# GpSimd takes over a quantiser's rounding, and two pieces of work are asked for earlier

## The chip, the cores and the metric

The kernel runs on one core of a Trainium2 chip. The core has a matrix engine (TensorE, PE in the profile, with its weight loads as PEld), VectorE (DVE), ScalarE (ACT), GpSimd (POOL) and SyncE (SP, which here issues DMA transfers). Each engine runs its own list of instructions strictly in order, so an instruction that waits holds up everything behind it in that list. The metric is the device time of one execution in microseconds (us).

## The reference

The input is x, two sequences of 4096 tokens with 512 channels. Two layers follow each other, and each adds two branches to its input.

```python
xn = _layernorm(x, axis=-1)
x = x + _L0_attn_ref(xn, ...) + _L0_ffn_ref(xn, L0_ffn_weight, L0_ffn_bias)
xn = _layernorm(x, axis=-1)
x = x + _L1_attn_ref(xn, ...) + _L1_ffn_ref(xn, ...)
```

In layer 0 the "attention" is two projections (w1, v1), a depthwise convolution of three taps with SiLU, a state-space recurrence over the tokens, a gate and a projection w2. Its "ffn" is a product of two quantised operands: every block of 32 numbers is divided by a scale and rounded to the nearest number of a 6-bit grid.

```python
scales = jnp.maximum(jnp.max(jnp.abs(blocks), axis=-1) / FP6_E2M3_MAX, eps)
q = _nearest_on_grid(blocks / scales[..., None], _GRID)
xd = (xq * xs[..., None]).reshape(x2.shape)   # wd likewise
out = xd @ wd.T + bias
```

In layer 1 the attention is linear: q and k through ReLU, the sums of k times v and of k over all tokens, a product with q, a quotient, and a layernorm of the result plus its input. Its ffn mixes each token with the one before it, `xk = mu_k * x + (1.0 - mu_k) * x_prev` and xr likewise, and computes `sigmoid(xr W_r) * (square(relu(xk W_k)) W_v)`.

## The kernel before, in words

Tokens are cut into blocks of 512, sixteen in all and eight in each sequence; a block holds four tiles of 128 tokens. Channels come in four groups of 128. Most operands are 128 x 512 numbers in 32-bit floats. The profile's times show these stages:

- the conv stage, to about 402 us: block by block the layer norm, the two projections, the taps (L479) and the stores for the recurrence. Beside the blocks, 24 of the 64 tiles and the 4 rows of the ffn weight are quantised (`beside`, `beside_block`);
- the recurrence, to about 620 us;
- the mixed blocks of sequence 0 (about 623 to 890 us): the gate, the products with w2 and with the quantised weight, the sum into x (L799 empties a bank of accumulators into x), the turned x for layer 1, and k (L894) with its running sum over tokens on GpSimd (L853). Eight more tiles are quantised here;
- the outer sums of k and v (about 890 to 992 us), with eight tiles (`early`) beside them; GpSimd prepares operands for them at L934;
- the pairs (about 992 to 1192 us): q and then k of layer 1's ffn for two blocks at a time, with products by seven quarter products (`seven`, L1072). ScalarE's L1079 copies a finished bank away, so that TensorE can go on; L1108 and L1109 finish q, L1119 to L1121 finish k. The remaining tiles of sequence 1's first blocks are quantised here (`later`);
- layer 1 of sequence 0 (about 1192 to 1450 us), with four tiles of sequence 1 beside it (`ahead`, through `at_block`);
- the mixed blocks, outer sums, pairs and layer 1 of sequence 1.

To quantise a tile, ScalarE normalises it (L136, four instructions), VectorE takes the largest magnitude in each block of 32 (L187), makes the scales (L188) and their reciprocals (L192); GpSimd multiplies by the reciprocals (L193); VectorE adds a small constant and writes the sum as an 8-bit float, which does the rounding (L201); GpSimd multiplies by the scales (L202); VectorE transposes the tile (L458; L445 for a weight row). SyncE stores most of the tiles (L460). The work is a generator of four steps, which other stages call a step at a time. The tiles share a ring of eight buffers (`yv`) with other temporaries, and a single buffer (`t2q`) holds a transposed tile until its store has landed.

The mixing for W_k (`mixed_k`) takes one instruction on ScalarE (L1138) and one on VectorE (L1139) for each group of channels of each of two blocks, sixteen instructions in all. It is called from `halfway`, between the fourth and fifth of q's seven products. The mixing for W_r (L1148, L1149) comes after q.

A framework's scheduler puts the instructions into each engine's list in an order that follows the program's, and adds the waits; so a change in the program also moves instructions that it does not touch.

Of the kernel before, what the change touches and what calls it, by code (L numbers as in the profile page):

```python
# [17 lines left out]
P = 128  # L18
# [26 lines left out]
def block_kernel(ctx: ExitStack, tc: tile.TileContext, a: dict, out: bass.AP):  # L45
# [152 lines left out]
    def mx_rounded(y, s):  # L198

        q = small.tile([P, D], FP8, tag="mx_q", name="mx_q")  # L200
        nc.vector.tensor_scalar(q, y, -LOWER * GRID, None, ALU.add, saturate=False)  # L201
        nc.gpsimd.tensor_tensor(  # L202
            by_block(y), by_block(q), s.unsqueeze(2).to_broadcast([P, NQ, QB]), ALU.mult
        )
# [405 lines left out]
    def t8(shape=(P, CC, T)):  # L610
        return cl.tile(list(shape), F32, tag="t8", name="t8", bufs=7)
# [414 lines left out]
    def quarters(w):  # L1026
        return lambda i, j: w[:, 2 * j : 2 * j + 2, i * 2 * P : (i + 1) * 2 * P]
# [73 lines left out]
    def pairs(b, xnTs, wq, wk, made, kvx, later):  # L1101

        xks = {}

        def put_q(p, o, n, pm, addend):
            t = t2("q")
            if addend is not None:
                nc.vector.tensor_tensor(t, pm, addend, ALU.add)  # L1108
            nc.scalar.activation(  # L1109
                t, pm if addend is None else t, AF.Relu, bias=bq[:, o, :]  # L1110
            )
            nc.scalar.dma_start(out=qd[b * NB + 2 * p + n, o], in_=t)
            if p:
                stepped(later)

        def put_k(p, o, n, pm, addend):
            t = t2("k")
            if addend is not None:
                nc.vector.tensor_tensor(t, pm, addend, ALU.add)  # L1119
            nc.scalar.activation(t, pm if addend is None else t, AF.Relu)  # L1120
            nc.scalar.activation(t, t, AF.Square)  # L1121
            nc.scalar.dma_start(out=kd[b * NB + 2 * p + n, o], in_=t)
            if p:
                stepped(later)

        def of_q(p):
            return [lambda k, n=n: xnTs[2 * p + n][:, k, 1 : T + 1] for n in range(2)]

        def of_k(p):
            return [lambda k, n=n: xks[p][n][:, k, :] for n in range(2)]  # L1130

        def mixed_k(p):
            xks[p] = [t8(), t8()]
            for n in range(2):
                xnT = xnTs[2 * p + n]
                for c in range(CC):
                    dst = xks[p][n][:, c, :]
                    nc.scalar.activation(dst, xnT[:, c, 0:T], AF.Copy, scale=om_k[:, c, :])  # L1138
                    nc.vector.scalar_tensor_tensor(  # L1139
                        dst, xnT[:, c, 1 : T + 1], mu_k[:, c, :], dst, ALU.mult, ALU.add  # L1140
                    )

        def mixed_r(p):
            for n in range(2):
                xnT = xnTs[2 * p + n]
                for c in range(CC):
                    t = yv.tile([P, T], F32, tag="yv", name="t")
                    nc.scalar.activation(t, xnT[:, c, 0:T], AF.Copy, scale=om_r[:, c, :])  # L1148
                    nc.vector.scalar_tensor_tensor(  # L1149
                        xnT[:, c, 1 : T + 1], xnT[:, c, 1 : T + 1], mu_r[:, c, :], t,  # L1150
                        ALU.mult, ALU.add,
                    )

        NP = NB // 2
        ts = token_sums(*of_q(0))
        sq = weight_sums(quarters(wq))
        sk = None
        for p in range(NP):

            def halfway():  # L1160
                nonlocal ts_k
                if p == 0:
                    keys_values(*made, kvx)
                mixed_k(p)
                ts_k = token_sums(*of_k(p))

            ts_k = None
            seven(quarters(wq), sq, *of_q(p), ts, ("mm", "tr", "acc"), partial(put_q, p), halfway)
            if p == 0:
                sk = weight_sums(quarters(wk))  # L1170
            mixed_r(p)

            def halfway():
                nonlocal ts
                if p + 1 < NP:
                    ts = token_sums(*of_q(p + 1))

            seven(quarters(wk), sk, *of_k(p), ts_k, ("acc", "tr", "mm"), partial(put_k, p), halfway)
            del xks[p]
        while later:  # L1180
            stepped(later)

    def layer1(b, xrs, mvs, kvx, wts, at_block):
        wr, wv = wts
        for i in range(NB):
            n = b * NB + i
            at_block(i)
            qT = t8()
            nc.sync.dma_start(out=qT, in_=qd[n].rearrange("c p t -> p c t"))
            xt8 = x8()  # L1190
            xt = [xt8[:, j, :] for j in range(TJ)]
            for j in range(TJ):
                nc.sync.dma_start(out=xt[j], in_=xd1[n, j * P : (j + 1) * P])
            ka = t8()
            nc.sync.dma_start(out=ka, in_=kd[n].rearrange("c p t -> p c t"))
            xr = xrs[i]
            y = t8((P, TJ, D))
            rs = []
            for j in range(TJ):
                tj = slice(j * P, (j + 1) * P)  # L1200
                for c2 in range(2):
                    pc = bank(("tr", "mm")[j % 2])[:, 0 : 2 * (P + HG)]
                    pc = pc.rearrange("p (c m) -> p c m", c=2)
                    for c in range(2):
                        nc.tensor.matmul(  # L1205
                            pc[:, c, :],
                            lhsT=qT[:, 2 * c2 + c, tj],
                            rhs=kvx[:, 2 * c2 + c, :],
                            start=True,
                            stop=True,  # L1210
                        )
                    den = small.tile([P, 2, HG], F32, tag="den", name="den")
                    nc.vector.tensor_scalar(den, pc[:, :, P:], EPS_DEN, None, ALU.max)
                    nc.vector.reciprocal(den, den)
                    nc.vector.tensor_tensor(
                        y[:, j, c2 * 2 * P : (c2 + 1) * 2 * P].rearrange(
                            "p (c h d) -> p c h d", c=2, d=HD
                        ),
                        pc[:, :, 0:P].rearrange("p c (h d) -> p c h d", d=HD),
                        den.unsqueeze(3).to_broadcast([P, 2, HG, HD]),  # L1220
                        ALU.mult,
                    )
                xn = t2("xn")
                rescaled(xn, xt[j], mvs[:, i, j, :])
                nc.vector.tensor_tensor(y[:, j, :], y[:, j, :], xn, ALU.add)
                nc.gpsimd.tensor_tensor(xt[j], xt[j], beta, ALU.add)  # L1226
                pr = acc()
                product(
                    pr, lambda k: xr[:, k, 1 + j * P : 1 + (j + 1) * P], lambda k: wr[:, k, :]
                )  # L1230
                r = t2("r")
                nc.scalar.activation(r, pr, AF.Sigmoid)  # L1232
                rs.append(r)
            mv = small.tile([P, TJ, 2], F32, tag="mv", name="mv")
            layernorm_stats(lambda j: y[:, j, :], mv)
            for j in range(TJ):
                tj = slice(j * P, (j + 1) * P)
                nc.vector.scalar_tensor_tensor(
                    y[:, j, :], y[:, j, :], mv[:, j, 0:1], gamma, ALU.subtract, ALU.mult
                )  # L1240
                nc.vector.scalar_tensor_tensor(
                    xt[j], y[:, j, :], mv[:, j, 1:2], xt[j], ALU.mult, ALU.add
                )
                pf = acc()
                product(pf, lambda k: ka[:, k, tj], lambda k: wv[:, k, :])
                nc.vector.tensor_tensor(rs[j], rs[j], pf, ALU.mult)  # L1246
                nc.vector.tensor_tensor(xt[j], xt[j], rs[j], ALU.add)
                nc.sync.dma_start(
                    out=out[b, i * T + j * P : i * T + (j + 1) * P, :], in_=xt[j]
                )  # L1250


    mv0 = const.tile([P, NK, TJ, 2], F32, name="mv0")
    eight = banks()

# [153 lines left out]
    for b in range(B):  # L1409
# [22 lines left out]
                quantised((b + 1) * NB, j, lambda j=j: xd0[j], t2q) for j in range(TJ)  # L1432
            ]

        def at_block(i):

            if b + 1 < B:
                for _ in range(2):
                    next(ahead[i // 2])
            if b + 1 < B and i == NB - 1:  # L1440
                next_in.append(t8())
                for cc in range(CC):
                    gated(b + 1, 0, next_in[0], cc)
# [70 lines left out]
```

## Time and profile before

| what | us |
|---|---|
| median of 3 runs | 2314.48 (2311.11 to 2317.88) |
| the profiled execution | 2317.41 |
| its span in the profile | 2315.6 |
| TensorE busy | 2261.1 (98%) |
| VectorE busy | 1587.5 (69%) |
| ScalarE busy | 1024.2 (44%) |
| GpSimd busy | 544.5 (24%) |

The mean clock that TensorE was granted is 0.992 of its full speed. A busy TensorE is given in the profile by modelled ends of its instructions. A line like `PE p_mm L781 <- DVE x L799: 15.7, 5, 4.8` says that TensorE, before an instruction of line 781 that writes p_mm, stood idle 15.7 us in five waits, the longest 4.8, and that VectorE's instruction of line 799 writing x ended them. In a timeline each line has the start, the duration, engine, line, operation, the written and the read names, their shapes, and in brackets the idle time of that engine just before and what ended it; consecutive instructions of one kind may be joined in a line (x2).

### The profile page before, as it was taken

To read this page: it belongs to the slowest core of one execution; us is meant where nothing else is said; L and a number is where in the kernel's file an instruction comes from. 1 tells how busy PE (TensorE), PEld (TensorE's weight loads), DVE (VectorE), ACT (ScalarE), POOL (GpSimd) and SP (SyncE) were. 2 spreads that over 40 slices of the span, in tenths; PEclk is the share of its full clock that TensorE was granted. 3 is DMA by queue.
4 is the path that set the end of the run, shared out by engine and by line. 5 is a ranking of instruction groups with operands and counts; after the bars stand their busy time and mean duration, and the time that the engine had idled before them with its cause. 6 is when DMAs were issued, how large, how long until landed. Compare 5 with 4: busy or idle time off the path is not lost. (4 is left out here: it accounts for less than half of the span.)

```text
span 2315.6 us, 24940 instructions
## 1 busy us (share of the span) xinstructions
PE 2261.1 (98%) x7648; PEld 1269.6 (55%) x7648; DVE 1587.5 (69%) x3115; ACT 1024.2 (44%) x2019; POOL 544.5 (24%) x548
## 2 busy tenths in 40 slices
PE   7999998999989999999999999999999999999999
PEld 3444443455467676854445555567676854445554
DVE  6788678655686764577668779677764355667777
ACT  5787775555232234357652222132132246652222
POOL 0013131011343225712012112333234600001111
PEclk9999999999999999999999999999999999999999
DMA  7854643389776557524274336457557412254431
GB/s 248 295 162 150 185 152 139 125 264 320 269 211 227 178 178 229 174 86 150 96 252 160 118 138 204 164 179 240 169 160 218 146 51 96 87 209 146 145 125 57
DMA packets 291766, 399.62 MB, mean 173 GB/s; under 512 B 59057, under 2 KB 120497, under 8 KB 290609
## 3 DMA queue, kind: packets, MB, share of 16 engines
q1 hardware_dynamic: 262544, 330.91, 43.9%
q10 hardware_dynamic: 29088, 67.12, 7.6%
q8 instruction: 61, 1.00, 0.2%
q14 instruction: 73, 0.59, 0.1%
HBM read 249.42 MB, written 148.53 MB: 172 GB/s over the span
## 5 line engine op out<-in xcount | busy, mean ns | idle before, releaser
L165 PE MATMUL p_acc<-w_W_v,t 128*128 128x512 f32 x512 | 222.3, 592 | 0.0
L1226 POOL TENSOR_TENSOR x<-x,row_beta 128x512 f32<-128x512 f32 x64 | 83.2, 1300 | 590.4 <-ACT xn L136 590.4
L165 PE MATMUL p_acc<-w_W_r,xnT 128*128 128x512 f32 x448 | 201.4, 592 | 0.0
L193 POOL TENSOR_TENSOR xq<-xq,mx_rs 128x512 f32<-128x512 f32 x64 | 69.7, 1093 | 438.9 <-DVE mx_rs L192 182.4
L165 PEld LDWEIGHTS p_acc<-w_W_v,t 128*128 128x128 f32 x512 | 97.3, 190 | 122.5 <-issue 119.8
L1232 ACT ACTIVATE r<-p_acc 128x512 f32<-128x512 f32 x64 | 38.3, 598 | 261.6 <-PE p_acc L165 248.2
L853 POOL TENSOR_TENSOR ksum<-ksum,k 128x512 f32<-128x512 f32 x62 | 83.9, 1354 | 238.6 <-ACT k L895 238.5
L136 ACT ACTIVATE xq<-xq,mvi 128x128 f32<-128x128 f32 x256 | 108.2, 483 | 69.6 <-DMA xq<-in_xi 38.2
L895 ACT ACTIVATE k<-k 128x512 f32<-128x512 f32 x64 | 40.3, 630 | 196.1 <-DVE k L894 185.3
L165 PEld LDWEIGHTS p_acc<-w_W_r,xnT 128*128 128x128 f32 x448 | 80.8, 190 | 80.4 <-issue 80.4
L118 ACT ACTIVATE rs_s<-rs_v 128x4 f32<-128x4 f32 (+1 forms) x41 | 8.4, 206 | 251.2 <-DVE rs_v L116 251.1
L479 DVE SCALAR_TENSOR_TENSOR xc<-x,col_conv_w,xc 128x512 f32<-128x512 f32 x128 | 99.4, 799 | 27.0 <-ACT xc L477 15.9
L781 PE MATMUL p_mm<-w_sums,t 128*128 128x256 f32 x416 | 100.7, 398 | 14.4 <-DVE x L799 14.4
L165 PE MATMUL p_acc<-xnT,w_w_w 128*128 128x512 f32 x224 | 102.6, 601 | 2.6 <-DVE xnT L333 1.9
L165 PE MATMUL p_acc<-xnT,w_v_w 128*128 128x512 f32 x224 | 100.8, 593 | 0.1
L165 PE MATMUL p_acc<-w_Wk,xnT 128*128 128x512 f32 x224 | 100.7, 592 | 0.0
L165 PE MATMUL p_tr<-w_Wk,xnT 128*128 128x512 f32 x224 | 100.7, 592 | 0.0
L131 DVE BATCH_NORM_STATS2 st<-x 128x6 f32<-128x512 f32 x128 | 84.1, 678 | 22.9 <-DMA x<-in_x 21.9
L781 PEld LDWEIGHTS p_mm<-w_sums,t 128*128 128x128 f32 x416 | 83.1, 201 | 28.4 <-DVE x L799 16.0
L1246 DVE TENSOR_TENSOR r<-r,p_acc 128x512 f32<-128x512 f32 x64 | 43.8, 685 | 75.7 <-PE p_acc L165 75.7
L781 PE MATMUL p_acc<-w_sums,t 128*128 128x256 f32 x416 | 94.0, 379 | 0.0
L136 ACT ACTIVATE xi<-xi,mvi 128x128 f32<-128x128 f32 x208 | 89.4, 482 | 9.1 <-DMA xq<-in_xi 3.0
(294 smaller groups left out, 4959.3 us busy)
## 6 DMA issues: line engine op xcount, KB each, us to landing
x<-in_x SPq DMA_DIRECT2D x126, 256.0 KB, 5.8
xq<-in_xi SPq DMA_DIRECT2D x64, 256.0 KB, 3.9
vd<-v ACTq DMA_DIRECT2D x64, 256.0 KB, 2.4
cd<-xs SPq DMA_DIRECT2D x64, 256.0 KB, 2.1
xg<-cd SPq DMA_DIRECT2D x16, 1024.0 KB, 8.0
v<-vd SPq DMA_DIRECT2D x64, 256.0 KB, 5.2
xd<-x SPq DMA_DIRECT2D x64, 256.0 KB, 2.3
ktd<-k SPq DMA_DIRECT2D x64, 256.0 KB, 2.4
```

Of the source, the lines that this page charges most:

```text
L118: nc.scalar.activation(s, v, AF.Sqrt)
L131: nc.vector.bn_stats(st[:, j, :], xt(j))
L136: nc.scalar.activation(dst, src, AF.Identity, bias=mv[:, 0:1], scale=mv[:, 1:2])
L165: nc.tensor.matmul(out_ap, lhsT=lhsT(k), rhs=rhs(k), start=(k == 0), stop=(k == CC - 1))
L193: nc.gpsimd.tensor_tensor(by_block(y), by_block(y), rs.unsqueeze(2).to_broadcast([P, NQ, QB]), ALU.mult)
L479: nc.vector.scalar_tensor_tensor(xc, x1[:, tap : tap + T], conv_w[:, cc, tap : tap + 1], xc, ALU.mult, ALU.add,)
L781: nc.tensor.matmul(po[:, u * 2 * P : (u + 1) * 2 * P], lhsT=x(k)[:, c, u, :], rhs=w(k)[:, c, :], start=first and k == 0 and c == 0 and u == 0,
L853: nc.gpsimd.tensor_tensor(ksum, ksum, kt, ALU.add)
L895: nc.scalar.activation(kt, kt, AF.Relu)
L1226: nc.gpsimd.tensor_tensor(xt[j], xt[j], beta, ALU.add)
L1232: nc.scalar.activation(r, pr, AF.Sigmoid)
L1246: nc.vector.tensor_tensor(rs[j], rs[j], pf, ALU.mult)
```

## The change

Three parts. First, the rounding in `mx_rounded` is done by GpSimd instead of VectorE: an addition of two tensors, the second a column of one number for each partition (`lower`), repeated along the row. Second, `mixed_k` takes a list of blocks; the first block of a pair is mixed ahead of q's seven products, the second where both were mixed. Third, `at_block` in layer 1 is called twice for each block, once at its start, ahead of the block's own loads, and once after the sigmoids; each call takes one step of a tile, and the operands for the next sequence's first gate are asked for in the first call of the last block.

```diff
-        nc.vector.tensor_scalar(q, y, -LOWER * GRID, None, ALU.add, saturate=False)
+        nc.gpsimd.tensor_tensor(
+            q, y, lower.to_broadcast([P, D]), ALU.add, saturate=False
+        )
...
-        def mixed_k(p):
-            xks[p] = [t8(), t8()]
-            for n in range(2):
+        def mixed_k(p, ns):
+            if p not in xks:
+                xks[p] = [t8(), t8()]
+            for n in ns:
...
-                mixed_k(p)
+                mixed_k(p, (1,))
                 ts_k = token_sums(*of_k(p))
 
             ts_k = None
+            mixed_k(p, (0,))
             seven(quarters(wq), sq, *of_q(p), ts, ("mm", "tr", "acc"), partial(put_q, p), halfway)
...
-            at_block(i)
+            at_block(i, 0)
             qT = t8()
...
                 rs.append(r)
+            at_block(i, 1)
             mv = small.tile([P, TJ, 2], F32, tag="mv", name="mv")
...
+    lower = const.tile([P, 1], F32, name="lower")
+    nc.gpsimd.memset(lower, -LOWER * GRID)
...
-        def at_block(i):
+        def at_block(i, half):
 
             if b + 1 < B:
-                for _ in range(2):
-                    next(ahead[i // 2])
-            if b + 1 < B and i == NB - 1:
+                next(ahead[i // 2])
+            if b + 1 < B and (i, half) == (NB - 1, 0):
```

## The prediction

> **What bounds the kernel now.** I read the page's busy row first, then what TensorE waited for, then the timelines around its waits. The page:
>
> ```profile
> span 2315.6 us, 24940 instructions
> ...
> PE 2261.1 (98%) x7648; PEld 1269.6 (55%) x7648; DVE 1587.5 (69%) x3115; ACT 1024.2 (44%) x2019; POOL 544.5 (24%) x548
> ```
>
> TensorE (PE) is the bound, and the change leaves its list of instructions as it is. So only its 54.5 us of idle time can move, and the stretches where its clock is halved. 9.5 us of the idle lie before the first matmul and 4.7 after the last. What ended the rest is in the list of TensorE's waits (total, times, longest):
>
> ```profile
> PE p_mm L781 <- DVE x L799: 15.7, 5, 4.8
> PE p_acc L1072 <- ACT t L1079: 5.4, 4, 2.6
> PE p_acc L1072 <- ACT x L364: 4.7, 1, 4.7
> PE p_mm L1072 <- ACT t L1079: 3.6, 1, 3.6
> ```
>
> The table by stretches (TensorE's busy time, number; weight loads; VectorE; ScalarE; GpSimd; clock) shows layer 1 without a gap, so part 3 can save nothing in it, while the end of the conv stage (370 to 406) and the mixed blocks of sequence 0 (623 to 710) lose 9.9 and 9.8 us:
>
> ```profile
> 370.00:406.00 36.00, 26.10 (x52) 10.60 (x51) 28.66 (x52) 16.77 (x36) 1.27 (x1) 0.91 0.33 117
> 623.00:710.00 87.00, 77.16 (x274) 54.55 (x275) 68.01 (x121) 29.46 (x71) 41.89 (x37) 0.92 0.62 193
> 1192.00:1450.00 258.00, 258.00 (x789) 130.29 (x788) 206.50 (x491) 75.66 (x110) 54.82 (x43) 1.00 0.47 164
> ```
>
> The next timeline (VectorE, start and length; idle time and its end in brackets) shows how the first row arises at 645 us:
>
> ```profile
> 643.90 0.43 DVE L201 TENSOR_SCALAR mx_q<-xq 128x512 fp8e4<-128x512 f32 x1 [0.34 <-POOL xq L193]
> 644.45 0.25 DVE L192 RECIPROCAL mx_rs<-mx_s 128x16 f32<-128x16 f32 x1
> 647.71 0.43 DVE L201 TENSOR_SCALAR mx_q<-xq 128x512 fp8e4<-128x512 f32 x1 [3.01 <-POOL xq L193]
> 648.06 0.68 DVE L894 TENSOR_TENSOR k<-p_tr,row_bk 128x512 f32<-128x512 f32 x1
> 648.66 0.68 DVE L799 TENSOR_TENSOR x<-x,p_mm 128x512 f32<-128x512 f32 x1
> ```
>
> The rounding L201 waits 3.01 us for GpSimd, and L799, which empties the bank that TensorE wants from 644.69, stands behind it. GpSimd in that stretch, where the second tile's L193 has to let L202 and the key sum L853 (which waits for ScalarE's k) go first:
>
> ```profile
> 642.50 1.37 POOL L193 TENSOR_TENSOR xq<-xq,mx_rs 128x512 f32<-128x512 f32 x1 [0.86 <-DVE mx_rs L192]
> 644.41 1.05 POOL L202 TENSOR_TENSOR xq<-mx_q,mx_s 128x512 f32<-128x512 fp8e4 x1 [0.54 <-DVE mx_s L188]
> 645.41 1.26 POOL L853 TENSOR_TENSOR ksum<-ksum,k 128x512 f32<-128x512 f32 x1
> 646.63 1.05 POOL L193 TENSOR_TENSOR xq<-xq,mx_rs 128x512 f32<-128x512 f32 x1
> ```
>
> **Part 1, the rounding.** 68 times (64 tiles, 4 weight rows) VectorE loses an operation of 0.60 us (mean of L201, 0.43 median) and GpSimd gains one. Before shows no such GpSimd operation. Bounds: 0.43 (VectorE's own) to 1.6 (the longest L202). Nearest are L193 and L202, same size, one broadcast operand: median 1.05, start to start 1.01. I take 1.05. A lone tile's chain from L193 to L202 took 2.64 (1.05, 0.03 to hand over, 0.43, 0.08, 1.05) and becomes 3 x 1.01 + 0.04 = 3.07, so 0.4 longer. But nothing on VectorE waits midway any more; L458 alone, at the end, still does.
>
> The Trainium skill, "GPSIMD Engine Reference", 4.1 Engine selection, speaks against this: two-input elementwise work belongs on VectorE, about twice as fast. The rows agree on the price (0.60 against 1.05); charged per operation it would make the change cost 68 x 0.45 = 31 us. It would only be so if these engines bounded the kernel, and the busy row says they do not.
>
> *Sequence 0's mixed blocks (623 to 710).* Two stalls, 4.70 at 644.69 and 4.80 at 690.15, each followed by 6.83 us at half clock (3.4 lost): 8.1 each. Gaps of up to 1.62 us are followed by full clock in this trace. In the changed order the second sequence of L188 and L192 and one L894 (0.17 + 0.25 + 0.68) stand between 643.6 and L799, so it starts at about 644.7 and ends 645.3: a gap of 0.7 without the half clock stays, -7.4. The second L799 (694.22) loses its own 2.08 wait + 0.43, and three earlier L201 (1.48, 1.26, 0.43 with waits of 0.72, 0.34, 0.59: 4.8), against up to 2 of L458 waiting longer: start 688.9 to 690; needed at 690.15. I count -5.6 for residue. Together -13; bounds -16 (all) and -5 (L458's waits take the place).
>
> *Sequence 1's mixed blocks.* The stalls of 1.33 at 1545.94 and 0.42 at 1571.63 are also L799 behind L201; they go: -1.7. The 4.49 one at 1485.95 hangs on loads and stores of tiles; L799 comes perhaps 0.5 earlier, with its share of half clock -0.8. Sum -2.5 (-4 to +1).
>
> *Conv stage (50 to 402).* It holds 28 of the 68. There L201 kept VectorE 14.5 busy and 8.8 waiting; 23.3 go. GpSimd gains 28 x 1.05 = 29. ScalarE must empty TensorE's banks behind this pipeline; the margin before TensorE stops falls to 0.05 us at 231 and 0.44 to 0.97 at 351 to 361, and is gone at 377, where 14.8 are lost in all. At 337 two tiles and two weight rows come at once: twelve GpSimd operations from 337.54 end about 349.7, and in the changed order a second L445 and L458 stand before L479, which moves from 346.40 to about 350.5 (+4.1, 3.5 above the margin). Against it the pair at 363 gains 0 to 0.7 and VectorE has fewer operations before. The most that can come back is 14.8, the most I see lost two bursts of 4.1; I take +1.5, between -8 (half of the 14.8) and +8, nearer to nothing than to either end because the two effects on VectorE oppose each other.
>
> Beside GpSimd's operations L201 took 1.25 instead of 0.43, and L763, with two tiles read, 1.76 instead of 0.68. The Trainium skill, "SBUF — State Buffer", Who interferes with whom, has the rule for it: an operation of VectorE with two SBUF inputs and one of GpSimd shut each other out for a whole instruction. Taken at its worst it would add 28 x 1.05 = 29 to VectorE here, 6 more than the 23.3 that go, and make the conv term +6. I stay at +1.5: L201's median is 0.43 and its mean 0.60, so such meetings are the exception.
>
> *Outer sums (924 to 982).* Eight tiles' worth, +8 on a GpSimd that TensorE follows closely. Adding the rows up in the changed order, the L934 that ended at 958.90 ends near 961 (TensorE about +2), but L458 and so the stores and xg loads queued on SyncE behind them come earlier, so the 1.0 to 1.6 lost at 955 and 970 go. +0.5 (-1.6 to +2.5).
>
> **Part 2, half of the mixing earlier.** Per pair of blocks, four of the eight L1138 on ScalarE (0.72) and L1139 on VectorE (0.75) go ahead of q's products. No work is added. The first four stand before gt's L980 to L985 on VectorE, at most 4 x 0.67 = 2.7 later; gt was done at 993.2 and TensorE takes it at 1006.1, so that hides it. Their two buffers of the ring of seven are taken earlier; a wait for them would stand as L1138 <- PE in ScalarE's queue, ahead of L1079. At 1110 ScalarE showed:
>
> ```profile
> 1110.33 0.72 ACT L1109 ACTIVATE q<-q,col_bq 128x512 f32<-128x512 f32 x1 [2.20 <-DVE q L1108]
> 1112.08 0.57 ACT L1079 COPY t<-p_acc 128x512 f32<-128x512 f32 x1
> 1112.55 1.33 ACT L1138 ACTIVATE t<-xnT,om_k 128x512 f32<-128x512 f32 x2
> 1113.78 0.57 ACT L1079 COPY t<-p_mm 128x512 f32<-128x512 f32 x1
> ```
>
> TensorE waited 3.59 for that last L1079. In the changed order no L458 (which waited 1.59 for its store) stands between the two L1108 on VectorE, and ScalarE, with as many mixing steps between its L1079 as before, follows the second L1108: that L1079 ends about 1112.1 instead of 1114.35, -2.2, and most of the half clock behind it (3.41 us, 1.7 lost) goes: -3.3. The stalls at 1034.76 and 1038.23 (1.49, 0.71) follow from L201's waits on VectorE and L1138 on ScalarE: both go, -2.2. At 1085.57: -0.5. The one at 1188.48 (2.55 and 1.7 of clock) waits for a tile's load queued on SyncE behind W_r and W_v; **part 3** puts one tile's load before those, but a later tile takes the old place in both queues: 0 (-4.3 to 0). The y and v loads for sequence 1, which it also asks for earlier, pass only stores and loads of layer 1, whose 258 us hide them: 0. Sum -3.3 - 2.2 - 0.5 = -6; bounds -11 and +2 (a load of a tile not landed when ScalarE comes to it earlier).
>
> **Sum.** -13 - 2.5 + 1.5 + 0.5 - 6 = -19.5. The profiled run took 2317.41 (span 2315.6 and 1.8 around it), 2.9 above the median of 2314.48. So 2297.9 from the one and 2295.0 from the other; between them I take 2296.
>
> **Rivals.**
> *Slower: VectorE's conv work queues behind L458.* Blocks 7 to 14 quantise two to five tiles each. If all eight bursts cost the 4.1 of 337, that is +33 in place of +1.5: 2296 + 31 = 2327. It decides from 5 bursts up (20 lost). For: the margins of 0.05 to 0.97. Against: 23.3 us less on VectorE.
> *The wait is only renamed.* L458 stands before later L799 and L747 and now waits for three operations. Then the two mixed terms (15.5) mostly come back: 2311. For: L458 already waited 0.94 and 0.30 at 367. Against: it stands behind the L799 that stalls TensorE at 645 and 690.
> *All goes well.* Conv takes -8 and the 1188 stall goes: 2296 - 9.5 - 4.3 = 2282.
> That the change does not do what it says is excluded for the rounding: in the order of instructions VectorE has 68 fewer, GpSimd 68 more and one memset.
>
> **How the numbers follow.** Forecast 0.47 (own range 2288 to 2306), slower rival 0.23, renamed wait 0.17, all well 0.13. 0.3% is 7 us, about what a measurement here can tell from none: below 2307.5 lie forecast, all well and 0.05 of the renamed wait, 0.65; above 2321.4 most of the slower rival, 0.21; between, 0.14. Range 2282 to 2324.
>
> **What would show it.** Right: TensorE's row for L799 falls from 15.7 to 5 or 6; no DVE L201 left; a POOL L201 near 1.05; L1079's 3.6 below 1.5. Wrong: L201 on POOL at 1.4 or more; TensorE's waits between 230 and 405 above 12 us (10 now); new rows of DVE L458 <- POOL L202 in front of L799 or L479.

## The result, and the profile after

The changed kernel took 2330.71 us (median of 4, 2327.21 to 2331.52), the kernel before beside it 2312.90: a ratio of 1.0071, with a 95% interval from 1.0051 to 1.0091. It is 17.8 us slower where 18.5 faster had been forecast (2296 from 2314.48), and it lies above the range, which ended at 2324. Here and below, differences in us are between medians; the ratios and their intervals are the record's own estimate and need not agree with them to the last digit. The two profiled executions differ by less, 2330.22 against 2317.41, since the one of before lay 4.5 above its median and this one 0.5 below its own.

Line numbers after L202 are two higher in the changed kernel: L204 is the product with the scales, L460 and L447 the transposes of a tile and of a weight row, L481 the taps, L801 what empties a bank into x, L936 the operands of the outer sums, and L944, L1055, L1081, L1121 and L1142 answer to L942, L1053, L1079, L1119 and L1139. The page's span and busy row after:

```profile
span 2328.1 us, 24957 instructions
...
PE 2267.6 (97%) x7648; PEld 1274.5 (55%) x7648; DVE 1581.4 (68%) x3047; ACT 1021.0 (44%) x2017; POOL 623.4 (27%) x617
```

VectorE lost 68 instructions and 6.1 us of busy time, not the 40.6 us that L201 had taken; GpSimd gained 69 and 78.9 us. TensorE's waits after:

```profile
PE p_mm L783 <- DVE x L801: 11.0, 4, 4.6
...
PE p_acc L1074 <- ACT t L1081: 7.9, 3, 3.2
PE p_tr L964 <- POOL t L936: 4.7, 1, 4.7
PE p_acc L165 <- ACT x L366: 4.0, 2, 3.2
PE p_mm L165 <- ACT x L366: 3.7, 1, 3.7
...
PE p_tr L165 <- ACT x L366: 2.7, 1, 2.7
```

The row of L801, which the forecast was built on, fell from 15.7 to 11.0 only. New are three rows of L165 waiting for L366 (ScalarE emptying banks in the conv stage; between 50 and 370 us TensorE had idled 0.1 us in all before) and one wait for GpSimd's L936. The stretches, in the same columns as before the change (their bounds are of the clock, and work has moved through them):

```profile
50.00:370.00 320.00, 309.55 (x707) 136.04 (x707) 234.38 (x423) 234.25 (x546) 95.32 (x89) 0.98 0.56 178
370.00:406.00 36.00, 30.36 (x68) 12.55 (x66) 27.29 (x56) 17.52 (x38) 7.96 (x7) 0.97 0.42 146
905.00:992.00 87.00, 82.26 (x344) 67.26 (x345) 44.07 (x63) 32.73 (x60) 66.22 (x68) 0.96 0.52 176
```

TensorE idles 10.5 us in the first row, where it had been busy 319.91 of 320, and 4.7 in the last, where it had idled 1.2.

Because TensorE runs the same 7648 matmuls in the same order in both kernels, its start times can be compared one by one. How late the changed kernel's TensorE is, at the end of each stage:

| at the end of | us late | in this stage |
|---|---|---|
| conv stage (405 us before) | 13.7 | +13.7 |
| mixed blocks of sequence 0, after the stalls at 645 and 690 | 6.5 | -7.2 |
| outer sums (992.36 us before, 1004.55 after) | 12.2 | +5.7 |
| pairs (up to 19.0 on the way) | 12.2 | 0.0 |
| layer 1, and all of sequence 1 | 12.5 | +0.3 |

(Two of the expectations below give this table's steps as 7.8 won back and 6.9 lost, and the lateness at 992 us as 12.9; the start times give the numbers here.) One such profile carries some noise: in runs described below that leave the conv stage as it is, TensorE stood 0 to 7 us earlier at 405 us than in the profile of before. The experiments therefore compare medians.

What happens in the conv stage is shown by VectorE's timeline at the burst of two tiles and two weight rows. Before, from the reciprocals of the weight rows to the first taps behind the burst:

```profile
337.47 0.36 DVE L192 RECIPROCAL mx_rs<-mx_s 128x16 f32<-128x16 f32 x2
...
346.40 0.74 DVE L479 SCALAR_TENSOR_TENSOR xc<-x,col_conv_w,xc 128x512 f32<-128x512 f32 x1
```

After:

```profile
349.27 0.37 DVE L192 RECIPROCAL mx_rs<-mx_s 128x16 f32<-128x16 f32 x2
...
354.43 0.71 DVE L460 STREAM_TRANSPOSE wide<-xq 128x512 f32<-128x512 f32 x1 [1.31 <-POOL xq L204]
355.44 0.71 DVE L447 STREAM_TRANSPOSE w_d<-w_y 128x512 f32<-128x512 f32 x1 [0.29 <-POOL w_y L204]
360.44 0.71 DVE L447 STREAM_TRANSPOSE w_d<-w_y 128x512 f32<-128x512 f32 x1 [4.30 <-POOL w_y L204]
361.45 0.71 DVE L460 STREAM_TRANSPOSE c<-xq 128x512 f32<-128x512 f32 x1 [0.29 <-POOL xq L204]
362.08 0.71 DVE L481 SCALAR_TENSOR_TENSOR xc<-x,col_conv_w,xc 128x512 f32<-128x512 f32 x1
```

No L201 is left, but the transposes wait 6.2 us for GpSimd's row of twelve operations, and the taps L481 stand behind them. L481 starts 12.8 us after the second L192 of the burst (349.27); before it was 8.9 (337.47 to 346.40). ScalarE waits 11.63 us for those taps, its L366 behind them comes late, and TensorE, whose banks L366 empties, stops for 3.74 us and then runs at half clock for a while; it is 6.6 us later behind this stall than before it:

```profile
362.83 0.63 ACT L488 ACTIVATE xc<-xc 128x512 f32<-128x512 f32 x1 [11.63 <-DVE xc L481]
365.91 2.93 PE L165 MATMUL p_mm<-xnT,w_w_w 128*128 128x512 f32 x3 [3.74 <-ACT x L366]
```

In the conv stage as a whole (50 to 402 us), VectorE's longest waits for GpSimd were, before and after:

```profile
DVE mx_q L201 <- POOL xq L193: 8.8, 12, 1.2
DVE c L458 <- POOL xq L202: 5.4, 6, 1.2
```

```profile
DVE c L460 <- POOL xq L204: 16.0, 12, 3.5
DVE w_d L447 <- POOL w_y L204: 7.5, 3, 4.3
DVE wide L460 <- POOL xq L204: 6.0, 4, 1.8
DVE xd L460 <- POOL xq L204: 4.8, 4, 1.5
```

### The profile page after: what moved, and what is told of

It reads as the page before. It is cut to its first block, busy times and chain, and to the rows that moved or that the text cites. A ratio compares the mean times of both kernels' runs of the same rounds, so it can differ in the third digit from the quotient of the medians.

```text
span 2328.1 us, 24957 instructions
## 1 busy us (share of the span) xinstructions
PE 2267.6 (97%) x7648; PEld 1274.5 (55%) x7648; DVE 1581.4 (68%) x3047; ACT 1021.0 (44%) x2017; POOL 623.4 (27%) x617
## 5 line engine op out<-in xcount | busy, mean ns | idle before, releaser
L165 PE MATMUL p_acc<-w_W_v,t 128*128 128x512 f32 x512 | 222.3, 593 | 0.0
L165 PE MATMUL p_acc<-w_W_r,xnT 128*128 128x512 f32 x448 | 201.4, 593 | 0.0
L165 PEld LDWEIGHTS p_acc<-w_W_v,t 128*128 128x128 f32 x512 | 97.5, 190 | 122.2 <-issue 119.1
L165 PEld LDWEIGHTS p_acc<-w_W_r,xnT 128*128 128x128 f32 x448 | 80.9, 190 | 80.2 <-issue 80.2
L481 DVE SCALAR_TENSOR_TENSOR xc<-x,col_conv_w,xc 128x512 f32<-128x512 f32 x128 | 100.5, 809 | 27.0 <-ACT xc L479 17.0
L165 PE MATMUL p_acc<-xnT,w_w_w 128*128 128x512 f32 x224 | 104.2, 610 | 7.3 <-ACT x L366 4.0
L165 PE MATMUL p_acc<-w_Wk,xnT 128*128 128x512 f32 x224 | 100.7, 593 | 0.0
L165 PE MATMUL p_tr<-w_Wk,xnT 128*128 128x512 f32 x224 | 100.7, 593 | 0.0
L165 PE MATMUL p_acc<-xnT,w_v_w 128*128 128x512 f32 x224 | 100.7, 593 | 0.0
L1074 PE MATMUL p_acc<-x,w_sums 128*128 128x512 f32 x192 | 90.4, 620 | 7.9 <-ACT t L1081 7.9
L777 POOL TENSOR_TENSOR x<-x,row_w_b 128x512 f32<-128x512 f32 x52 | 69.7, 1363 | 100.0 <-DMA x<-in_x 88.7
```

The source lines that it names most:

```text
L165: nc.tensor.matmul(out_ap, lhsT=lhsT(k), rhs=rhs(k), start=(k == 0), stop=(k == CC - 1))
L481: nc.vector.scalar_tensor_tensor(xc, x1[:, tap : tap + T], conv_w[:, cc, tap : tap + 1], xc, ALU.mult, ALU.add,)
L777: nc.gpsimd.tensor_tensor(xt[:, j, :], xt[:, j, :], b_out, ALU.add)
L1074: nc.tensor.matmul(banks[c], lhsT=lhsT(k, c), rhs=rhs(k), start=first and k == 0, stop=k == 1, skip_group_check=True,)
```

## The experiments

Theory A: moving the rounding costs, because what VectorE used to wait for at L201 it waits for at the transpose instead, one GpSimd operation later, and other work is queued there. Rival B: the two moved pieces cost. Each run below is set against the kernel before on the same chip. A tag tells which tiles round on GpSimd; the others round on VectorE as before:

```diff
-    def mx_rounded(y, s):
+    def mx_rounded(y, s, where):
...
+        if where in ON_GPSIMD:
+            nc.gpsimd.tensor_tensor(
+                q, y, lower.to_broadcast([P, D]), ALU.add, saturate=False
+            )
+        else:
+            nc.vector.tensor_scalar(q, y, -LOWER * GRID, None, ALU.add, saturate=False)
```

**The rounding alone.** Parts 2 and 3 of the change undone:

```diff
-                mixed_k(p, (1,))
+                mixed_k(p, (0, 1))
...
-            mixed_k(p, (0,))
...
-            at_block(i, 0)
+            at_block(i)
...
-            at_block(i, 1)
```

> The rounding on GpSimd alone; the mixing and layer 1 as before. Theory A (the rounding costs: VectorE's transposes of quantised tiles wait for three GpSimd operations in a row, and what stands behind them comes late; matching TensorE's instructions one by one, the changed kernel was 13.7 us late at the end of the conv stage, 7.8 were won back in sequence 0's mixed blocks and 6.9 lost in the outer sums): 12 to 18 us slower than before, as the whole change. Rival B (the pieces asked for earlier cost, the rounding is neutral as forecast or a gain): within 5 us of before or faster.

Measured: 2330.61 against 2312.65, ratio 1.0074 (1.0055 to 1.0094). The rounding carries the whole loss.

**The moved pieces alone.** The rounding undone:

```diff
-        nc.gpsimd.tensor_tensor(
-            q, y, lower.to_broadcast([P, D]), ALU.add, saturate=False
-        )
+        nc.vector.tensor_scalar(q, y, -LOWER * GRID, None, ALU.add, saturate=False)
```

> The two moved pieces alone, the rounding on VectorE as before. Theory A: within 5 us of before, since after the pairs and layer 1 the changed kernel stood where it stood before them (12.3 late at 1192 us, 12.9 late at 992). Rival B: 10 to 18 us slower. The prediction's own count for these moves was 6 us faster, together with the rounding in that stage.

Measured: 2313.85, ratio 1.0002 (0.9989 to 1.0015). Rival B falls; parts 2 and 3 are worth nothing that can be measured here, on the kernel before.

**Stage by stage: the conv stage.**

```diff
+ON_GPSIMD = ('conv', 'w')
```

> The rounding on GpSimd in the conv stage alone (24 tiles and 4 weight rows), nothing else changed. Theory A: TensorE 13 to 15 us late at 405 us, the total 12 to 16 us slower. Rival C (the conv stage only shifts waits, and most of its loss would be found again in a later stage that waits for something else, such as a load): total less than 6 us slower.

Measured: 2329.07, ratio 1.0068 (1.0048 to 1.0087), 16.4 us slower. In its profile TensorE was 12.2 late at 405 us, and of that only some 4 us were found again, at the start of sequence 1's mixed blocks. Rival C falls.

**The mixed blocks.**

```diff
+ON_GPSIMD = ('mixed',)
```

> The rounding on GpSimd for the sixteen tiles of the mixed blocks alone. Theory A with the second half of the prediction's mechanism: TensorE's waits for L799 fall from 15.7 to 9 to 11 us, total 6 to 10 us faster, nearly all of it in sequence 0. Rival D (the gain at 645 us needs the other stages' shift): within 3 us of before.

Measured: 2304.91, ratio 0.9965 (0.9953 to 0.9976): 7.7 us faster. TensorE's waits for L799 (L805 in this kernel) fell from 15.7 us to:

```profile
PE p_mm L787 <- DVE x L805: 11.1, 5, 4.0
```

So the gain in the mixed blocks is real, it does not depend on the other stages, and rival D falls.

**The outer sums.**

```diff
+ON_GPSIMD = ('early',)
```

> The rounding on GpSimd for the eight tiles beside the outer sums alone. Theory A (there GpSimd also prepares TensorE's operands at L934, and a tile's third operation stands in front of them in its list): TensorE waits once 4 to 5 us for POOL t, with half clock after it, total 5 to 8 us slower. Rival E (that wait came only because the conv stage and the mixed blocks had shifted the stores and loads): within 3 us of before.

Measured: 2318.36, ratio 1.0026 (1.0015 to 1.0037), 5.8 us slower. Its profile has the wait alone, of the same length as in the changed kernel:

```profile
PE p_tr L968 <- POOL t L940: 4.7, 1, 4.7
```

Rival E falls. In the changed kernel GpSimd's list there, and what TensorE does:

```profile
959.67 2.31 POOL L936 TENSOR_TENSOR t<-xg 128x256 f32<-128x256 f32 x2
961.95 1.18 POOL L936 TENSOR_TENSOR t<-t,xg 128x256 f32<-128x256 f32 x1
963.20 1.11 POOL L936 TENSOR_TENSOR t<-xg,t 128x256 f32<-128x256 f32 x1
964.28 1.04 POOL L193 TENSOR_TENSOR xq<-xq,mx_rs 128x512 f32<-128x512 f32 x1
965.40 1.04 POOL L201 TENSOR_TENSOR mx_q<-xq,lower 128x512 fp8e4<-128x512 f32 x1
966.52 1.04 POOL L204 TENSOR_TENSOR xq<-mx_q,mx_s 128x512 f32<-128x512 fp8e4 x1
967.52 1.41 POOL L936 TENSOR_TENSOR t<-xg 128x256 f32<-128x256 f32 x2
969.00 0.72 POOL L936 TENSOR_TENSOR t<-t,xg 128x256 f32<-128x256 f32 x1
```

```profile
964.01 1.03 PE L964 MATMUL p_tr<-t,t 128*128 128x256 f32 x4
969.78 2.08 PE L964 MATMUL p_tr<-t,t 128*128 128x256 f32 x4 [4.74 <-POOL t L936]
```

Half of the product runs on the first four L936; the other half needs the L936 that ends at 969.72, and a whole tile (three operations, 3.2 us) stands between the two. TensorE waits 4.74 and then runs four matmuls in 2.08 instead of 1.03, at half clock.

**Pairs and layer 1.**

```diff
+ON_GPSIMD = ('ahead', 'later')
```

> The rounding on GpSimd for the twelve tiles beside the pairs and the four beside layer 1 alone. Theory A with the lock on the port (VectorE's L1053 and L1139, which read two tiles, took 1.53 instead of 0.68 beside the row of GpSimd's operations): no gain or 1 to 5 us slower, although VectorE has 16 operations less. The prediction's mechanism (no waits of L201 in front of L1108 and L1119): 2 to 6 us faster.

Measured: 2312.49, ratio 1.0001 (0.9991 to 1.0010). No gain, as theory A had it, though VectorE has 16 operations less. In the changed kernel VectorE's list and GpSimd's run in step here:

```profile
1036.47 2.98 DVE L1055 TENSOR_TENSOR x<-t,x 128x512 f32<-128x512 f32 x2
1039.37 0.70 DVE L460 STREAM_TRANSPOSE mx_c<-xq 128x512 f32<-128x512 f32 x1
1039.99 2.36 DVE L1142 SCALAR_TENSOR_TENSOR t<-xnT,col_mu_k,t 128x512 f32<-128x512 f32 x2
```

```profile
1035.96 1.49 POOL L204 TENSOR_TENSOR xq<-mx_q,mx_s 128x512 f32<-128x512 fp8e4 x1
1037.41 1.48 POOL L201 TENSOR_TENSOR mx_q<-xq,lower 128x512 fp8e4<-128x512 f32 x1
1038.86 1.49 POOL L193 TENSOR_TENSOR xq<-xq,mx_rs 128x512 f32<-128x512 f32 x1
```

Two L1055, which took 0.68 each, take 2.98; GpSimd's operations take 1.49 instead of 1.05. The transpose L460, with one tile to read, keeps its 0.70. The run of the pairs and layer 1 has such a row too (three of these operations in 1.52 to 1.53 each, at 1020 to 1025 us). Whether this lock is what swallowed the gain was not tried by itself.

The ratios of the four stages (+0.68, -0.35, +0.26, +0.01%) add up to +0.60%, against +0.74% (0.55 to 0.94) for the rounding as a whole.

**What in the conv stage costs: GpSimd's time without the chain.** In the kernel before, after L202:

```diff
+        if where in ("conv", "w"):
+            spare = small.tile([P, D], FP8, tag="spare", name="spare", bufs=1)
+            nc.gpsimd.tensor_tensor(
+                spare, q, lower.to_broadcast([P, D]), ALU.add, saturate=False
+            )
```

> The kernel before, and after each of the 28 quantised tiles or weight rows of the conv stage GpSimd does one addition more, of the same size and kinds of numbers, into a tile that nobody reads. It keeps GpSimd as busy as the change does, and holds the port as often, but no chain waits for it except a next tile's. Theory A1 (what costs is that the tile's own chain to VectorE's transpose is one GpSimd operation longer): within 4 us of before. Theory A2 (what costs is GpSimd's time itself, by the port or by the next tile behind it): 8 us slower or more.

Measured: 2320.06, ratio 1.0040 (1.0025 to 1.0055), 7.5 us slower: between the two. The transposes do not account for it: VectorE's waits for GpSimd between 50 and 402 us grew only from 21.9 to 24.0 us. VectorE's busy time over the whole kernel grew by 3.2 us, with as many operations; what the rest consists of is not shown.

**The transposes put off.** On top of the conv stage's rounding on GpSimd, the last step of each tile is called in the next block:

```diff
             def beside_block(n):
                 nonlocal xd_b1
+                while put_off:
+                    put_off.pop(0)()
                 for what, j in beside.get(n, ()):
+                    if len(put_off) == 4:
+                        put_off.pop(0)()
...
-                        quantise(what, j, None)
+                        put_off.append(quantise(what, j, None))
```

> The rounding on GpSimd in the conv stage, as in the run of that stage alone, but each tile's transpose is put off to the next block, so that it stands behind that block's taps in the program. Theory A1 (taps queued behind a transpose that waits for GpSimd): most of the 16 us comes back, total within 5 us of before. Theory A2 (port or GpSimd's time): 10 us slower or more.

Measured: 2328.24, ratio 1.0073 (1.0057 to 1.0090). Nothing came back; by its expectation theory A2. But the edit did not do what it was for. The transposes' waits for GpSimd between 50 and 402 us, in the run with the conv stage alone:

```profile
DVE c L464 <- POOL xq L208: 16.1, 12, 3.5
DVE w_d L451 <- POOL w_y L208: 7.5, 3, 4.3
DVE wide L464 <- POOL xq L208: 6.0, 4, 1.8
DVE xd L464 <- POOL xq L208: 3.3, 3, 1.5
```

They sum to 32.9 us, and the same four rows of this run to 35.8 (19.1, 5.3, 6.9 and 4.5): the transposes still wait. The run tells nothing of the two.

**The chain cut.** As many GpSimd operations as with the conv stage's rounding, but the transpose waits for the first alone:

```diff
+        out = y
+        if where in ("conv", "w"):
+            out = small.tile([P, D], FP8, tag="spare", name="spare", bufs=1)
         nc.gpsimd.tensor_tensor(
-            by_block(y), by_block(q), s.unsqueeze(2).to_broadcast([P, NQ, QB]), ALU.mult
+            by_block(out), by_block(q), s.unsqueeze(2).to_broadcast([P, NQ, QB]), ALU.mult,
+            saturate=False,
         )
```

> The rounding on GpSimd in the conv stage, as many GpSimd operations as there, but the product with the scales is written into a tile that nobody reads, so that the transpose waits for the first of the three operations alone (what it leaves out: the quantised operand of these tiles is neither rounded nor scaled back). VectorE has its 28 operations less. Theory A1 (the cost is VectorE's wait for the second and third operation): VectorE's idle time ended by GpSimd in the stage falls from 40 to below 15 us, total 2 to 12 us faster than before. Theory A2 (the cost is GpSimd's time and the port): 5 us slower or more. The additional operations off the chain cost 7.5 us, so a mixture would end within 5 us of before.

Measured: 2311.23 against 2312.83, ratio 0.9995 (0.9985 to 1.0004), 1.6 us faster. The same rows:

```profile
DVE c L468 <- POOL xq L194: 4.5, 3, 2.0
DVE wide L468 <- POOL xq L194: 2.6, 3, 1.2
DVE xd L468 <- POOL xq L194: 1.9, 3, 0.7
DVE w_d L455 <- POOL w_y L194: 0.9, 3, 0.3
```

With these waits at 9.9 us instead of 32.9, 16.4 us slower becomes 1.6 faster, a difference of 18.0, though every engine has as many operations as in the conv stage's run. TensorE's waits for the banks that ScalarE empties (L370; L374 in this kernel) fell with it, from 15.8 us to 1.6. So the wait for the second and third operation is what carries the loss. The 18.0 is not the increase against the kernel before: there the transposes waited 8.8 us and L201 another 8.8 for GpSimd, so the chain here is shorter than in either kernel. Of the two theories neither holds alone, since GpSimd's time is not free (7.5 us in the run of the spare operations). One sum through the three medians is: GpSimd's time and port +7.5, VectorE's 28 operations and their waits at L201 gone -9.1 (-1.6 less 7.5), the transposes' wait +18.0; together +16.4. Three runs always fit three terms. The sum takes for granted that the terms add, the middle one is what is left over and was not measured by itself, and by the runs' intervals each is uncertain by some 3 to 5 us.

**Versions that might beat both.** The mixed blocks alone on GpSimd, with both moved pieces:

```diff
+ON_GPSIMD = ('mixed',)
```

> The rounding on GpSimd in the mixed blocks alone, with both moved pieces. If the parts add up: the 7.7 us of the mixed blocks and nothing (0.9966 of before). More than 10 us faster would mean that the moves help once the mixed blocks are quicker.

Measured: 2304.29 against 2312.83, ratio 0.9953 (0.9935 to 0.9972). And the changed kernel with the conv stage and the outer sums back on VectorE:

```diff
+ON_GPSIMD = ('ahead', 'later', 'mixed')
```

> The changed kernel with the rounding of the conv stage and of the outer sums back on VectorE; the mixed blocks, pairs and layer 1 round on GpSimd, and both moved pieces stay. If the parts add up: as the mixed blocks alone, 6 to 9 us faster than before, and some 25 us faster than the changed kernel. If the pairs' operations hold VectorE by the port: 2 to 5 us less of it.

Measured: 2305.60, ratio 0.9967 (0.9951 to 0.9982). With the mixed blocks alone these are three versions between 7 and 9 us faster than before and 25 to 26 us faster than the change; their intervals overlap, so the moves and the pairs add nothing that shows.

## Why the prediction was wrong

- **What bounds the kernel: right.** TensorE's instructions stayed, and all of the change is in its idle time and in the stretches of half clock behind waits.
- **The price of the operation: right.** 1.05 was taken; L201 on GpSimd has a median of 1.04 (1.03 to 1.51). It was not the operation's size that failed.
- **The step that failed, the conv stage: "There L201 kept VectorE 14.5 busy and 8.8 waiting; 23.3 go", net +1.5.** The run of this stage alone measured +16.4. The 14.5 went, the waiting did not: VectorE's idle time ended by GpSimd in this stage, all rows, rose from 21.9 to 41.9 us, so that VectorE lost 5.5 us where 23.3 were counted as won. The prediction wrote of part 1 that "L458 alone, at the end, still does" wait, and set no price on it; the run with the chain cut shows that this wait carries the loss (18.0 us between waiting for three operations and for one). The one burst that it worked out by hand was right, +4.1 forecast and +3.9 measured for the taps; it was then set off against the 23.3, and the others were counted only in a rival. What such a burst costs TensorE was too small as well, since half clock follows the longer waits: 4.1 was priced, 4.8, 5.8 and 6.6 were measured at 217, at 332 to 340 and at 362 us. At 217 two-input operations of VectorE were stretched too (L1039 1.54 instead of 0.69); they were stretched as much (1.53) in the run with the chain cut, which lost nothing there. The prediction's own sign of being wrong, TensorE's waits between 230 and 405 us above 12, came: 9.9 before, 12.8 after.
- **The rival that came true** is the slower one, priced 2327 by eight such bursts and given 0.23; 2330.7 was measured. Its place and its mechanism, VectorE's conv work queued behind the transposes, were right. That its number came close is luck: three bursts cost TensorE 17.2 us, of which 3.9 came back by 445 us, not eight that cost 33, and the 21 us of gains that the rival kept from the sum came to about 2 in the runs by stage (-7.7, +5.8 and nothing).
- **The outer sums, +0.5 (about +2 by GpSimd's row, less 1.0 to 1.6 by loads that come earlier): right place, half clock left out.** The row was seen (the L936 that answers to 958.90 ending near 961), but it ended at 969.72, which is 963.3 less the 6.5 that everything was late by. Of the 2.3 us between, 1.7 are the four L936 of the group before it, which took 4.6 (959.67 to 964.32) where the same four took 2.9 in the kernel before (950.35 to 953.25), beside VectorE's two-input L944. The loads gave back a little more than was counted, 2.0 us. But the wait of 4.74 cost 4.9, and the half clock behind it another 2.8, which the forecast did not have: +5.7 in this profile, +5.8 by the run alone.
- **The mixed blocks, -13 and -2.5: half of it.** The first stall went nearly as worked out, 4.70 to 1.27 (0.7 forecast), and TensorE won 6.0 us there (7.4 forecast). The second went from 4.80 to 3.71 only, and 1.4 was won (5.6 forecast). Its L801 came at 701.04, and on the way to it the transposes had waited 3.00 and 0.95 for GpSimd and 1.62 for a store:

```profile
681.38 0.71 DVE L460 STREAM_TRANSPOSE mx_c<-xq 128x512 f32<-128x512 f32 x1 [3.00 <-POOL xq L204]
...
689.14 0.71 DVE L460 STREAM_TRANSPOSE mx_c<-xq 128x512 f32<-128x512 f32 x1 [0.95 <-POOL xq L204]
...
701.04 0.63 DVE L801 TENSOR_TENSOR x<-x,p_mm 128x512 f32<-128x512 f32 x1
```

  That looks like the second rival, the wait renamed, for one of the two stalls; two L635 stretched beside GpSimd's key sum (2.13, where two L633 had taken 1.53) are on the way as well. In sequence 1 the wait of 4.49 stayed at 4.64, and TensorE won nothing in all, where -2.5 was forecast. The run of the mixed blocks alone puts both sequences at -7.7; its one profile shows 5.2 won in sequence 0 and 1.1 in sequence 1.
- **Parts 2 and 3 and the pairs, -6: nothing.** The stall of 3.59 at 1110 went, as worked out, but others grew: 1.49 to 2.35 at 1047, 0.65 to 3.20 at 1099, where ScalarE waited 5.03 for L1121 on VectorE behind the stretched operations. The 2.2 counted for the stalls at 1034.76 and 1038.23 rested in part on a wrong reading: the mixing step among ScalarE's copies there is L1148, which part 2 does not move, and not L1138, and the second of them waited for a transpose of VectorE:

```profile
1034.99 0.72 ACT L1148 ACTIVATE t<-xnT,om_r 128x512 f32<-128x512 f32 x1
...
1037.69 0.72 ACT L1148 ACTIVATE t<-xnT,om_r 128x512 f32<-128x512 f32 x1 [1.50 <-DVE mx_c L458]
```

  Part 3 at nothing was right. So was the claim that the earlier mixing in front of gt is hidden: TensorE's lateness stayed at 12.2 from 992 to 1030 us.
- **The page against the change.** The Trainium skill, "GPSIMD Engine Reference", 4.1 Engine selection, was set aside because these engines do not bound the kernel; that stays true of their busy time. Its advice held for the change as a whole, by waits, and not for the mixed blocks, which gained 7.7 us against it.

What stays open: how the second mixed stall divides between L460's waits and the stretched operations beside GpSimd, what GpSimd's 7.5 us in the conv stage consist of, and whether the transposes could be ordered so that the taps pass them (the one attempt did not remove the waits). The order of each engine's list also differs a little from kernel to kernel, so a difference between two runs can hold some of that too.

## What to carry to other kernels

When an operation is moved off an engine, do not count what the engine waited there as won: in this case the wait went to the next instruction that needs the same chain. The chain's new length has to be priced there, with all that is queued behind it, in every place where it occurs. The same edit won 7.7 us in one stage and lost 16.4 in another, where the margin was nearly gone; an edit in a shared helper is worth trying stage by stage. An instruction list that is identical in two kernels (TensorE's here) gives a ledger of the loss by stage at once, within the noise of one profile.

## What the runs showed of the hardware

When an operation of VectorE that reads two tiles and GpSimd's operations both come in a row, each slows the other: at 1034 to 1039 us L1055 took 1.43 to 1.53 us for 0.68, and GpSimd's operations 1.48 to 1.50 for 1.05, at the same rhythm, while VectorE's transpose of one tile kept 0.70. The Trainium skill, "SBUF — State Buffer", Who interferes with whom, has the second to come wait for the whole of the first. The rows agree that both are held up, and that the transpose is not. L201 in the kernel before read one tile too, and took 1.25 beside GpSimd's operations as the prediction noted, which the rule for two inputs that it quoted does not cover. If nothing overlapped, each round would take 1.01 + 0.60 = 1.61 us (an estimate from the start-to-start times of such operations alone); the rows show a round each 1.45. GpSimd's 28 additional operations in the conv stage, with nothing but a next tile waiting for them, cost 7.5 us; how much of that is this lock and how much their place in GpSimd's list was not separated.
